# Keys and values of a non-local attention layer: splitting 192 channels as 128 and 64 instead of 96 and 96

## The chip, the core and the metric

The kernel runs on one core of one Trainium2 chip. A core has five engines that run at the same time, each through its own list of instructions: TensorE (PE in the profile, with PEld for the loading of its stationary operand), VectorE (DVE), ScalarE (ACT), GpSimd (POOL) and SyncE (SP), which here issues most of the DMA transfers. The metric is the device time of one execution in microseconds, as a median of several runs.

## The reference

A batch of 4 images with C = 192 channels and 64 x 64 pixels passes through four layers. Layer 0 is an attention block whose queries come from a deformable convolution, with an MLP. Layer 1 is the non-local attention that the change touches. Layer 2 is an attention over overlapping windows with a gated MLP, and layer 3 a depthwise 3 x 3 convolution whose weights depend on the image. Layer 1, with 96 inner channels and N = 4096 pixels:

```python
g_x     = _conv1x1(x, g_w, g_b).reshape(B, O, N)          # O = 96
theta_x = _conv1x1(x, theta_w, theta_b).reshape(B, O, N)
phi_x   = _conv1x1(x, phi_w, phi_b).reshape(B, O, N)
f1 = jnp.einsum('bon,bom->bnm', theta_x, phi_x)
f_div_C = jax.nn.softmax(f1, axis=-1)
y = jnp.einsum('bnm,bom->bon', f_div_C, g_x).reshape(B, O, H, W)
return _conv1x1(y, W_w, W_b) + x
```

So for each image the keys phi (96 x 4096) and the values g (4096 x 96) have to be there in full before the first score can be weighted.

## The kernel before

An image is worked through layer by layer, and the four images follow one another. All data are float32. A matmul on TensorE contracts over partitions: `lhsT` is loaded as the stationary operand and `rhs` is streamed through it. In float32 each matmul appears in the trace as two PE instructions.

**Keys and values.** `keys(b, ph, gx, sb, ps)` makes them for image b. It goes over the 4096 pixels in NCH = 8 chunks of CN = 512. For each chunk one DMA (L865) loads the tile `xk` with the 192 channels as two groups of P = 96 partitions. Two matmuls (L868) contract over 96 + 96 channels and give 96 x 512 of phi in one PSUM bank (`tp`). ScalarE adds the bias and writes it into `ph` (L869). Eight matmuls (L873) give g with pixels on the partitions: four blocks of 128 pixels, each contracted over 96 + 96 channels, side by side in one bank (`g`). VectorE copies them into `gx` (L876). Then the generator yields.

**Who runs beside it.** For images 0 and 3 the chunks follow one another alone, with 4 buffers for `xk`. For images 1 and 2 the driver alternates chunk by chunk with `offsets(b + 1)`, the norm and the offset convolution of the next image's layer 0, with 2 buffers. `offsets` loads its own chunk `xi` (L431), takes mean and variance on TensorE (L360 pm, L339 pv, with ScalarE's squares L367), turns them back into rows (L348 pb), transposes the normed pixels (L462 pt) into a table in DRAM (L466) and writes the normed image (L471). When all eight chunks are done it runs the convolution for the offsets (L482 po, L490 pp) and computes the sampling positions (L494) and indices (L515). After it, `layer1` runs for image b: theta (L912), scores (L920), softmax and weighting (L986). Woven into it is the gather of the next image by indirect DMAs on GpSimd (L572). [...]in images 1 and 2 `offsets` holds 6 and `keys` has 2 (pool `l1kps`).

**The order on each engine.** The program is written as generators in a fixed order, but a list scheduler then orders the instructions of all engines, with tile pools deciding when a buffer is free. DMAs that are given to `in_turn` keep their written order. The weights of layer 1 (`phiT`, `gT`) are loaded by `late()` in `constants()` (L178), one DMA each, on SP's queue.

**Names that come up.** `M`, `Q` = 128, 64; `HN` = 256; `half(q)` = the partitions 64q to 64q + 63; `bass.ts(i, n)` = columns i n to (i + 1) n. fc1 of the MLP (`mlp0`, L803 and L810) contracts over 192 channels as 128 and 64. L693 is a matmul that does no work of the reference: it is issued in idle stretches of TensorE. L1787 and L1793 are layer 3's sums on VectorE and its output stores on SP, which for images 1, 2 and 3 are the last work ahead of `keys`.

Of the kernel before, what the change touches and what calls it, by code (L numbers as in the profile page):

```python
# [10 lines left out]
F32 = mybir.dt.float32  # L11
I32 = mybir.dt.int32
AF = mybir.ActivationFunctionType
ALU = mybir.AluOpType
AX = mybir.AxisListType
PSUM = bass.MemoryType.PSUM
DRAM = bass.MemoryType.DRAM

B, C, H, W = 4, 192, 64, 64
HW = H * W  # L20
P = 96
# [3 lines left out]
M, Q = 128, 64  # L25
NCH = 8
CN = HW // NCH
HN = CN // 2
# [51 lines left out]
def conv_seq_kernel(ctx: ExitStack, tc: tile.TileContext, a, out: bass.AP):  # L80
    nc = tc.nc

    def pool_of(**kw):

        return tc.tile_pool(**({} if kw.get("space") == DRAM else {"reuse_waits": "tile"}), **kw)
# [7 lines left out]
    def const(shape, name):  # L93
        return wpool.tile(shape, F32, tag=name, name=name)
# [8 lines left out]
    V, VW = {}, {}  # L103
    at = 0
# [67 lines left out]
    def in_turn(dma):  # L172

        tc.keep_in_program_order(dma)

    def late(name, src):
        t = const(list(src.shape), name)
        in_turn(nc.sync.dma_start(out=t, in_=src))  # L178
        return t

    def constants():
# [4 lines left out]
        at = 0  # L186
# [2 lines left out]
            at += m * n  # L189

        yield
        thetaT, phiT, gT = (late(n, a[n].rearrange("(k p) n -> p k n", p=P)) for n in ("thetaT", "phiT", "gT"))
        wW = late("wW", a["wW"])

        yield
# [27 lines left out]
        with pool_of(name="wideps", bufs=1, space=PSUM) as pp:  # L223
            n = sum(n for name, n in _V96 if name in _WIDE)
            wide = const([M, 2, n], "wide")
            p = pp.tile([M, 2, n], F32, tag="p", name="p_wide")
            at = 0
            for name, n in _V96:
                if name in _WIDE:
                    cols = slice(at, at + n)  # L230
# [13 lines left out]
        with pool_of(name="foldq", bufs=1, space=PSUM) as pp:  # L244
            p = pp.tile([128, 2, 512], F32, tag="p", name="p_qkv")
            n = 3 * C // 2
# [13 lines left out]
        with pool_of(name="outb", bufs=1, space=PSUM) as pp:  # L260
            p = pp.tile([P, 2], F32, tag="outb", name="pob")
# [6 lines left out]
        bias = const([128, 3, 2, WS * WS], "bias")  # L268
# [3 lines left out]
        with pool_of(name="rpb", bufs=1) as rp:  # L272
            shifted = rp.tile([WS, HEADS, N1 * N1], F32, tag="shifted", name="shifted")
            n = N1 * N1 - WS + 1
            for iy in range(WS):
                in_turn(nc.sync.dma_start(
                    out=shifted[iy : iy + 1, :, 0:n],
                    in_=a["rpb"][:, WS - 1 - iy : WS - 1 - iy + n].unsqueeze(0),
# [22 lines left out]
        for c in range(0, 32, HEADS):  # L301
            n = min(HEADS, 32 - c)
# [14 lines left out]
    with pool_of(name="zero", bufs=1) as zp:  # L317
        zero = zp.tile([128, 4 * C], F32, tag="zero", name="zero")
        nc.gpsimd.memset(zero, 0.0)
        for i in range(2):  # L320
            t = dram.tile([TROWS, 4 * C], F32, tag=f"table{i}", name=f"table{i}")
# [8 lines left out]
    x_flat = [dram.tile([C, HW], F32, tag=f"xd{i}", name=f"xd{i}") for i in range(2)]  # L330
    xn_drams, x_drams = ([t.rearrange("(k p) n -> p k n", p=P) for t in ts] for ts in (xn_flat, x_flat))
# [56 lines left out]
    def links(steps, upto=None):  # L388

        while True:  # L390
            try:
                link = next(steps)
                if upto is not None and link == upto:
                    return None
            except StopIteration as end:
                return end.value
# [462 lines left out]
    def keys(b, ph, gx, sb, ps):  # L859

        nc.gpsimd.memset(gx[:, :, P : P + 1], 1.0)
        for i in range(NCH):
            cols = bass.ts(i, CN)
            x = sb.tile([P, 2, CN], F32, tag="x", name=f"xk_{b}_{i}")
            nc.sync.dma_start(out=x, in_=x_drams[b % 2][:, :, cols])  # L865
            p = ps.tile([128, CN], F32, tag="k", name=f"tp_{b}_{i}")[:P]
            for k in range(2):
                nc.tensor.matmul(p, lhsT=phiT[:, k, :], rhs=x[:, k, :], start=k == 0, stop=k == 1)  # L868
            nc.scalar.activation(ph[:, cols], p, AF.Identity, bias=V["l1_phib"])  # L869
            p = ps.tile([128, CN], F32, tag="k", name=f"g_{b}_{i}")[:, : 4 * P].rearrange("p (j c) -> p j c", j=4)  # L870
            for j in range(4):
                for k in range(2):
                    nc.tensor.matmul(  # L873
                        p[:, j, :], lhsT=x[:, k, bass.ts(j, 128)], rhs=gT[:, k, :], start=k == 0, stop=k == 1
                    )
            nc.vector.tensor_copy(gx[:, bass.ts(i, 4), 0:P], p)  # L876
            yield


# [452 lines left out]
    def of_pair(x, j):  # L1332

        return x[:, bass.ts(j, UN)].rearrange("p (h n) -> p h n", h=2), x[:, 4 * UN + CN * j : 4 * UN + CN * j + CN]

    def half(h):
        return slice(Q * h, Q * h + Q)
# [458 lines left out]
    def rest(b, x, others, oi, sums, m2):  # L1796


        with ExitStack() as s:
            alone = m2 is None  # L1800
            sb = s.enter_context(pool_of(name="norms", bufs=1))
            ps = s.enter_context(pool_of(name="restps", bufs=2, space=PSUM))
            wide = s.enter_context(pool_of(name="restps2", bufs=5, space=PSUM))
            psums = Psums({"n": ps, "v": ps, "h": wide}, {"t": "h"})
            other = iter(())
            if not alone:
                other = mlp0(b + 1, m2, s.enter_context(pool_of(name="l0d", bufs=1)), sb, psums)
            credit = 0.0

            def main():  # L1810
                hn = []

                def ahead():
                    hn.append(links(pair_norm_steps(x, 0, sb, psums, f"l2n2_{b}_0")))

                yield from project(b, x, others, oi.pop(), psums, HFT_PE if alone else (), ahead)
                yield from mlp(b, x, sums, sb, psums, GATE_PE if alone else (), hn)
                yield from layer3(b, x, sums, psums, alone)

            for part in main():  # L1820
                credit += part
                while credit >= 1.0:
                    next(other, None)
                    credit -= 1.0
            for _ in other:
                pass

    def weave(b, at, m2):


        def begin(s):
            parts = gather(b, s, at, m2)
            done = 0

            def go(step):
                nonlocal done
                upto = GATHER_STEPS + 1 if step is None else min(GATHER_STEPS + 1, (GATHER_STEPS + 1) * step // (NQ * NG - 6))
                while done < upto:
                    done += 1
                    next(parts, None)  # L1840

            return go

        return begin
# [13 lines left out]
    with ExitStack() as s:  # L1858
        sb = s.enter_context(pool_of(name="l0first", bufs=1))
        m2 = stats.tile([M, C + 3 * M], F32, tag="m2", name="m2_0")  # L1860
        kept = sb.tile([128, NT, C], F32, tag="kept", name="kept")
        at = links(offsets(0, sb, kept))
# [11 lines left out]
    with ExitStack() as s:  # L1874
        sb, pool = (s.enter_context(pool_of(name=n, bufs=1)) for n in ("norms0", "l0d0"))
        ps = s.enter_context(pool_of(name="l0dps", bufs=2, space=PSUM))
# [3 lines left out]
    for b in range(B):  # L1880
        with ExitStack() as s:
            sb = s.enter_context(pool_of(name="l1x", bufs=1))
            ph = sb.tile([P, HW], F32, name=f"ph_{b}", tag="ph")
            gx = sb.tile([128, HW // 128, P + 1], F32, name=f"gx_{b}", tag="gx")
            beside, m2, at = None, None, at_second
            if b + 1 < B:
                m2 = stats.tile([M, C + 3 * M], F32, tag="m2", name=f"m2_{b + 1}")
            with ExitStack() as s2:
                making = keys(
                    b, ph, gx, s2.enter_context(pool_of(name="l1k", bufs=2 if 0 < b < B - 1 else 4)),  # L1890
                    s2.enter_context(pool_of(name="l1kps", bufs=2, space=PSUM)),
                )
                if 0 < b < B - 1:
                    parts = offsets(b + 1, sb)
                    for _ in range(NCH):
                        next(parts)
                        next(making, None)
                    at = links(parts)
                for _ in making:
                    pass  # L1900
            if b + 1 < B:
                beside = weave(b + 1, at, m2)
            layer1(b, (ph, gx), beside)
        begun.close()
        sums = stats.tile([M, 12], F32, tag="sums", name=f"sums_{b}")
        x = big.tile([M, UNITS * UN + 2 * 2 * 10 * (W + 2)], F32, tag="x", name=f"x_{b}")
        others = x[:, UNITS * UN :].rearrange("p (v k r c) -> p v k r c", v=2, k=2, c=W + 2)

        def load_image():
            for j in range(NCH // 2):  # L1910
                lo, hi = of_pair(x, j)
                for h in range(2):
                    of = x_flat[b % 2][:, bass.ts(2 * j + h, CN)]
                    nc.sync.dma_start(out=lo[:, h], in_=of[0:M])
                    nc.sync.dma_start(out=hi[half(h)], in_=of[M:C])

        oi = big.tile([P, 2, HW], F32, tag="x", name=f"oi_{b}")
        windows(b, oi, load_image)
        held = [oi]
        del oi  # L1920
        rest(b, x, others, held, sums, m2)
        del x, others
# [74 lines left out]
```

## Time and profile before

| | |
|---|---|
| median of 3 runs | 6832.62 us (6821.38 to 6850.82) |
| the profiled execution | 6953.4 us, span 6951.6 us, mean granted TensorE clock 0.938 |
| TensorE busy | 6255.4 us, 90% |
| VectorE, ScalarE, GpSimd busy | 69%, 54%, 30% |
| phi matmuls (L868), 128 instructions | 85.6 us busy |
| g matmuls (L873), 512 instructions | 82.7 us busy |
| `xk` loads (L865) | 32 of 384 KB |
| keys of image 0, alone | 859.9 to 907.7 us |
| keys of image 1 with offsets of image 2 | first phi at 2398.8 us, indices at 2514.4 us |
| keys of image 2 with offsets of image 3 | first phi at 4023.8 us, indices at 4134.2 us |
| keys of image 3, alone | 5640.2 to 5692.1 us |

All but the first row come from one profiled execution, which was 1.8% longer than the median. A share of the span is an average over very different stages; what matters for this change are the four stages in the last rows. A row such as `L868 PE MATMUL tp<-xk,phiT 96*96 96x512` names the line, the engine, the tiles written and read, the rows and columns of the stationary operand and the shape of the result. After it come the count, the busy time in us, the mean of one in ns, and how long the engine was idle just before these instructions and what ended that wait. Matmuls are pipelined, so a mean of 795 ns doesn't say that one can start only every 795 ns: the distance of their starts says that.

### The profile page before, as it was taken

Reading aid. Unit: us, or ns where it says so; the run is one execution under the profiler, and the core shown is the slowest. Engines: PE = TensorE matmul, PEld = TensorE weight load, DVE = VectorE, ACT = ScalarE, POOL = GpSimd, SP = SyncE. Lnnn points to the kernel's source line nnn. Section 1 sums busy time; section 2 is a strip of 40 time slices with the busy share of each in tenths; the row PEclk is TensorE's granted clock in tenths of the full one; section 3 lists DMA queues with packets and bytes.
Section 4 is the critical chain, followed back from the end, with each engine's and each line's share of the span. In section 5 each row is a group of like instructions: output and inputs, shape, how many; then the busy total and the mean of one; then the engine's idle time right before and its main releaser. Section 6 shows DMA issues by size and latency. Waiting matters only on the chain.

```text
span 6951.6 us, 115213 instructions
## 1 busy us (share of the span) xinstructions
PE 6255.4 (90%) x45188; PEld 4235.5 (61%) x45188; DVE 4817.8 (69%) x7087; ACT 3725.4 (54%) x6214; POOL 2061.6 (30%) x2273
## 2 busy tenths in 40 slices
PE   7677999999988899999988899999998889999876
PEld 4445578886643468886654458887554457766432
DVE  3664279985577769985586849996576757765656
ACT  3664368874544358874544348885544325545331
POOL 2654057752200047761200017772210000012100
PEclk8888989999999999999989999999998979999988
DMA  7795257751010277762010067673110010010000
GB/s 229 257 317 180 70 161 225 226 180 36 21 28 13 62 237 227 220 214 57 11 42 12 21 216 217 220 222 102 32 29 22 14 52 10 14 36 12 7 3 20
DMA packets 362109, 743.45 MB, mean 107 GB/s; under 512 B 52647, under 2 KB 245335, under 8 KB 360798
## 3 DMA queue, kind: packets, MB, share of 16 engines
q0 software_dynamic: 95616, 469.38, 21.1%
q1 hardware_dynamic: 265950, 266.70, 12.9%
q8 instruction: 356, 5.83, 0.4%
q14 instruction: 187, 1.53, 0.1%
HBM read 628.06 MB, written 106.21 MB: 106 GB/s over the span
## 4 chain that ended last, share of the span: by engine, by line
PE 65%; DVE 17%; ACT 7%; issue 4%; DMA 4%; SPq 1%; another core or an unknown queue 1%; POOL 1%; DVEq 0%; ACTq 0%; POOLq 0%
PE s L920 11%; PE y L986 11%; PE h L590 7%; PE v L1151 2%; DVE ha L1328 2%; PE qk L1076 2%; PE h L1528 2%; DMA ring<-table,idx 2%; PE qk L1077 2%; DVE ga L1328 2%; PE po L482 2%; PE t L1159 1%; PE h L803 1%; DVE gate L1328 1%; PE zm L1539 1%
## 5 line engine op out<-in xcount | busy, mean ns | idle before, releaser
L572 POOL DMA_INDIRECT ring<-table,idx x1188 | 1657.7, 1395 | 1103.3 <-DVE row L579 273.2
L920 PE MATMUL s<-ths,ph 96*128 96x256 f32 x4096 | 981.6, 385 | 14.2 <-ACT ths L914 7.4
L920 PEld LDWEIGHTS s<-ths,ph 96*128 96x128 f32 x4096 | 782.8, 193 | 154.8 <-ACT ths L914 19.0
L578 ACT ACTIVATE row<-ring,pos 128x384 f32<-128x384 f32 x1188 | 697.7, 609 | 213.5 <-DVE xo L583 132.4
L579 DVE SCALAR_TENSOR_TENSOR row<-ring,fr,row 128x384 f32<-128x384 f32 x1188 | 696.9, 611 | 84.1 <-ACT row L578 56.8
L986 PE MATMUL y<-sc,gx 128*97 128x256 f32 x3008 | 720.1, 379 | 0.0
L582 ACT ACTIVATE xo<-row,pos 128x192 f32<-128x192 f32 x1188 | 504.6, 448 | 151.3 <-remote 73.1
L986 PEld LDWEIGHTS y<-sc,gx 128*97 128x97 f32 x3008 | 489.0, 164 | 125.7 <-issue 2.3
L583 DVE SCALAR_TENSOR_TENSOR xo<-row,fr,xo 128x192 f32<-128x192 f32 x1188 | 464.4, 411 | 106.9 <-ACT xo L582 59.6
L590 PE MATMUL h<-ti,xo 128*128 128x192 f32 x2376 | 460.3, 329 | 5.6 <-DVE xo L583 5.6
L922 ACT COPY sc<-s 128x1024 f32<-128x1024 f32 x376 | 377.3, 1003 | 164.1 <-PE s L920 155.1
L983 DVE TENSOR_TENSOR sc<-sc,mbs 128x1024 f32<-128x1024 f32 x376 | 446.7, 1216 | 20.9 <-ACT mbs L946 13.7
L927 DVE TENSOR_TENSOR top<-top,sc 128x1024 f32<-128x1024 f32 x282 | 344.5, 1222 | 149.5 <-ACT sc L922 133.9
L590 PEld LDWEIGHTS h<-ti,xo 128*128 128x128 f32 x2376 | 404.4, 191 | 40.4 <-DVE xo L583 11.7
L984 ACT ACTIVATE sc<-sc 128x1024 f32<-128x1024 f32 x376 | 392.5, 1053 | 39.2 <-DVE sc L983 36.6
L1135 DVE TENSOR_REDUCE es<-ex 128x6 f32<-128x384 f32 x264 | 133.3, 546 | 358.8 <-ACT ex L1131 358.8
L590 PE MATMUL h<-kept,xo 128*128 128x192 f32 x990 | 261.9, 402 | 121.4 <-DVE xo L583 61.7
L1569 POOL COPY gate<-gate 128x192 f32<-128x192 f32 x12 | 4.2, 351 | 1115.2 <-ACT gate L1562 1115.2
L590 PEld LDWEIGHTS h<-kept,xo 128*128 128x128 f32 x990 | 191.2, 226 | 203.6 <-DVE xo L583 92.9
L1328 DVE SCALAR_TENSOR_TENSOR ga<-gate,v,ga 128x1024 f32<-128x1024 f32 x234 | 299.7, 1281 | 7.2
L986 PE MATMUL y<-se,gx 128*97 128x256 f32 x1088 | 260.4, 379 | 0.5 <-ACT yn L992 0.5
L1533 ACT ACTIVATE z<-h,bias_fc1T 128x512 f32<-128x512 f32 x192 | 118.0, 687 | 230.2 <-PE h L1530 229.9
(390 smaller groups left out, 11548.6 us busy)
## 6 DMA issues: line engine op xcount, KB each, us to landing
ti<-table SPq DMA_DIRECT2D x396, 96.0 KB
table<-tt SPq DMA_DIRECT2D x24, 1056.0 KB
ring<-table,idx POOLq DMA_INDIRECT x1188
xnd<-xn SPq DMA_DIRECT2D x4, 3270.0 KB
table<-kept SPq DMA_DIRECT2D x12, 1056.0 KB
table<-tt SPq DMA_DIRECT2D x44, 288.0 KB
xi<-in_x_dram SPq DMA_DIRECT2D x32, 384.0 KB
xk<-xd SPq DMA_DIRECT2D x32, 384.0 KB
```

Of the source, the lines that this page charges most:

```text
L572: nc.gpsimd.indirect_dma_start(out=gt.rearrange("p r q c -> p (r q c)"), out_offset=None, in_=table[:, :], in_offset=bass.IndirectOffsetOn ...
L578: nc.scalar.activation(row, gt[:, :, 0, :], AF.Copy, scale=pos[:, t, 9 + tap : 10 + tap])
L579: nc.vector.scalar_tensor_tensor(row, gt[:, :, 1, :], fr[:, t, 9 + tap : 10 + tap], row, ALU.mult, ALU.add)
L582: nc.scalar.activation(xo[:, j, :], row[:, 0, :], AF.Copy, scale=pos[:, t, tap : tap + 1])
L583: nc.vector.scalar_tensor_tensor(xo[:, j, :], row[:, 1, :], fr[:, t, tap : tap + 1], xo[:, j, :], ALU.mult, ALU.add)
L590: nc.tensor.matmul(acc[m // 2][:, bass.ts(m % 2, C)], lhsT=xo.rearrange("p j c -> p (j c)")[:, bass.ts(m, 128)], rhs=tt, start=t == 0 and ...
L920: nc.tensor.matmul(p[:, t, :], lhsT=ph[:, bass.ts(G * g + t, 128)], rhs=ths[i], start=True, stop=True)
L922: nc.scalar.copy(to, p)
L983: nc.vector.tensor_tensor(ex, ex, mbs[i].unsqueeze(1).to_broadcast([128, G, QN]), ALU.add)
L984: nc.scalar.activation(ex, ex, AF.Exp)
L986: nc.tensor.matmul(py, lhsT=gx[:, G * g + t, :], rhs=ex[:, t, :], start=g == 0 and t == 0, stop=g == NG - 1 and t == G - 1,)
L1328: nc.vector.scalar_tensor_tensor(acc[:, b], src(tap, b), w[:, tap : tap + 1], acc[:, b], ALU.mult, ALU.add)
```

## The change

The 192 channels are split as 128 and 64 instead of 96 and 96. Channels 0 to 127 of a chunk lie on all 128 partitions, 512 columns wide. Channels 128 to 191 of the chunk's first 256 pixels lie on partitions 0 to 63, those of its second 256 pixels on partitions 64 to 127, in 256 further columns. The weights are laid out in the same way, with the last 64 rows once on each half. So a chunk takes three loads instead of one, and the two weights take three each.

Phi becomes four matmuls of 256 columns: 128 channels for each half of the pixels, into two PSUM banks, and then 64 channels for each, on different halves of the partitions. g takes eight matmuls as before, for two blocks j: 128 channels for both halves, then 64 channels for both. Each result is in two banks, and so there are two evictions of half the size on ScalarE and two copies on VectorE. `l1kps` has 4 buffers for images 0 and 3, and 2, as before, for images 1 and 2.

```diff
@@ constants()
-        thetaT, phiT, gT = (late(n, a[n].rearrange("(k p) n -> p k n", p=P)) for n in ("thetaT", "phiT", "gT"))
+        thetaT = late("thetaT", a["thetaT"].rearrange("(k p) n -> p k n", p=P))
+        phiT, gT = const([M, 2, P], "phiT"), const([M, 2, P], "gT")
+        for t, n in ((phiT, "phiT"), (gT, "gT")):
+            in_turn(nc.sync.dma_start(out=t[:, 0, :], in_=a[n][0:M]))
+            for q in range(2):
+                in_turn(nc.sync.dma_start(out=t[half(q), 1, :], in_=a[n][M:C]))
@@ keys()
+        image = x_flat[b % 2]
         for i in range(NCH):
-            cols = bass.ts(i, CN)
-            x = sb.tile([P, 2, CN], F32, tag="x", name=f"xk_{b}_{i}")
-            nc.sync.dma_start(out=x, in_=x_drams[b % 2][:, :, cols])
-            p = ps.tile([128, CN], F32, tag="k", name=f"tp_{b}_{i}")[:P]
-            for k in range(2):
-                nc.tensor.matmul(p, lhsT=phiT[:, k, :], rhs=x[:, k, :], start=k == 0, stop=k == 1)
-            nc.scalar.activation(ph[:, cols], p, AF.Identity, bias=V["l1_phib"])
-            p = ps.tile([128, CN], F32, tag="k", name=f"g_{b}_{i}")[:, : 4 * P].rearrange("p (j c) -> p j c", j=4)
-            for j in range(4):
-                for k in range(2):
+            x = sb.tile([M, 3 * HN], F32, tag="x", name=f"xk_{b}_{i}")
+            nc.sync.dma_start(out=x[:, 0:CN], in_=image[0:M, bass.ts(i, CN)])
+            for q in range(2):
+                nc.sync.dma_start(out=x[half(q), CN:], in_=image[M:C, bass.ts(2 * i + q, HN)])
+            banks = [ps.tile([128, CN], F32, tag="k", name=f"tp_{b}_{i}_{q}")[:P, 0:HN] for q in range(2)]
+            for q, p in enumerate(banks):
+                nc.tensor.matmul(p, lhsT=phiT[:, 0, :], rhs=x[:, bass.ts(q, HN)], start=True, stop=False)
+            for q, p in enumerate(banks):
+                nc.tensor.matmul(p, lhsT=phiT[half(q), 1, :], rhs=x[half(q), CN:], start=False, stop=True)
+            for q, p in enumerate(banks):
+                nc.scalar.activation(ph[:, bass.ts(2 * i + q, HN)], p, AF.Identity, bias=V["l1_phib"])
+            banks = [
+                ps.tile([128, CN], F32, tag="k", name=f"g_{b}_{i}_{q}")[:, 0 : 2 * P].rearrange("p (j c) -> p j c", j=2)
+                for q in range(2)
+            ]
+            for j in range(2):
+                for q, p in enumerate(banks):
+                    at = HN * q + 128 * j
+                    nc.tensor.matmul(p[:, j, :], lhsT=x[:, at : at + 128], rhs=gT[:, 0, :], start=True, stop=False)
+                for q, p in enumerate(banks):
+                    at = CN + 128 * j
                     nc.tensor.matmul(
-                        p[:, j, :], lhsT=x[:, k, bass.ts(j, 128)], rhs=gT[:, k, :], start=k == 0, stop=k == 1
+                        p[:, j, :], lhsT=x[half(q), at : at + 128], rhs=gT[half(q), 1, :], start=False, stop=True
                     )
-            nc.vector.tensor_copy(gx[:, bass.ts(i, 4), 0:P], p)
+            for q, p in enumerate(banks):
+                nc.vector.tensor_copy(gx[:, bass.ts(2 * i + q, 2), 0:P], p)
             yield
@@ the driver
-                    s2.enter_context(pool_of(name="l1kps", bufs=2, space=PSUM)),
+                    s2.enter_context(pool_of(name="l1kps", bufs=2 if 0 < b < B - 1 else 4, space=PSUM)),
```

## Prediction

> **What bounds the kernel now.** I read the page's busy times first, to see which engine is short:
>
> ```profile
> span 6951.6 us, 115213 instructions
> PE 6255.4 (90%) x45188; PEld 4235.5 (61%) x45188; DVE 4817.8 (69%) x7087; ACT 3725.4 (54%) x6214; POOL 2061.6 (30%) x2273
> ```
>
> TensorE (PE) is 90% busy. That is an average, so next come the groups of the two lines that change, with shapes kept apart, and of the gated MLP's fc1 (L803, L810), which already works as the change would: 128 channels, then 64 on each half of the partitions.
>
> ```profile
> L868 PE MATMUL tp<-xk,phiT 96*96 96x512 f32 x128 | 85.6, 795 | 6.7 <-DMA xk<-xd 5.6 <-ACT ph L869 0.9
> L873 PE MATMUL g<-gT,xk 96*128 96x96 f32 x512 | 82.7, 328 | 0.0
> L869 ACT ACTIVATE ph<-tp,v 96x512 f32<-96x512 f32 x32 | 21.9, 683 | 159.6 <-PE tp L868 137.5 <-issue 17.1 <-PE g L873 5.0
> L803 PE MATMUL h<-d_l0m,fc 128*128 128x256 f32 x768 | 206.9, 413 | 16.7 <-DVE d_l0m L749 14.5 <-ACT z L1533 2.2
> L810 PE MATMUL h<-d_l0m,fc 64*128 64x256 f32 x768 | 113.3, 408 | 0.0
> ```
>
> The changed lines hold 85.6 + 82.7 = 168.3 us of PE: 2.4% of the span, so no outcome is large. ACT's eviction waits 137.5 us for PE and PE 0.9 us for ACT: PE sets the pace. The chain of waits says whether these stages are on the path, and what a chunk takes. First it passes L803/L810 ahead of image 0's keys, then two chunks, then (after "...") two later half-chunks:
>
> ```profile
> 840.16 1.92 PE h L803 x8
> 842.08 1.06 PE h L810 x8
> ...
> 860.08 1.72 PE tp L868 x4
> 861.80 1.76 PE g L873 x16
> ...
> 878.88 3.36 PE g L873 x16
> 882.24 3.41 PE tp L868 x4
> ```
>
> A chunk is 1.72 + 1.76 = 3.48 us early and 3.36 + 3.41 = 6.77 us later: same instructions, double time. The windows show why (the columns are sum, then PE, PEld, DVE, ACT, POOL busy, granted clock, DMA share, GB/s); image 0, image 3, image 1, image 2:
>
> ```profile
> 868.00:905.00 37.00, 36.74 (x104) 23.61 (x105) 3.35 (x6) 3.62 (x6) 0.94 (x1) 0.50 0.30 89
> 5650.00:5680.00 30.00, 30.00 (x90) 20.16 (x90) 2.79 (x5) 2.73 (x4) 0.00 (x0) 0.50 0.17 46
> 2412.00:2449.00 37.00, 36.50 (x249) 23.69 (x248) 17.74 (x24) 17.13 (x24) 0.00 (x0) 1.00 0.34 97
> 4022.00:4069.00 47.00, 45.15 (x284) 28.38 (x283) 18.90 (x25) 18.66 (x27) 0.00 (x0) 1.00 0.44 127
> ```
>
> PE is full in all four. Images 0 and 3 (keys alone, 859.9 to 907.7 and 5640.2 to 5692.1) run at clock 0.50; images 1 and 2, where chunks alternate with the offsets of the next image, run at 1.00. In images 1 and 2 the stage ends when PE has done the offset convolution, then L494, then the indices L515 (2514.4 and 4134.2), which release the first gather (2515.7 and 4135.6). So every PE microsecond in any of the four stages moves the end.
>
> [...]
>
> ```profile
> 5616.66 1.99 PE L803 MATMUL h<-d_l0m,fc 128*128 128x256 f32 x8
> 5618.59 1.13 PE L810 MATMUL h<-d_l0m,fc 64*128 64x256 f32 x8
> 5619.65 0.70 PE L803 MATMUL h<-d_l0m,fc 128*128 128x256 f32 x2
> ```
>
> Listed singly, the L810 instructions start in pairs 6 ns apart. So a pair takes one slot of 1.72/8 = 0.215 us (256 columns; 512 took 1.72/4). Eight slots and four slots would be 1.72 and 0.86 us, but the starts lie 1.93 and 1.06 us apart: **each switch between 128 and 64 rows costs 0.20 us**. [...] PE is full for 37 us at 0.50. [...]
>
> **The change part by part.** Per matmul PE runs two instructions (x16 for 8 matmuls of g).
>
> Removed: half of the streaming of 64 rows. In slots, phi was 4 x 0.43 = 1.72 us and becomes 4 + 2 slots of 0.215 = 1.29; g was 16 x 0.11 = 1.76 and becomes 12 x 0.1115 = 1.34. A chunk would be 2.63 instead of 3.48 us, 25% less.
>
> Added: switches. In the written order phi has 2, and g has 4. Phi's cost 0.20. For g the last-to-first gap in the trace between the shapes puts one near 0.16. Sum 0.40 + 0.64 = 1.04, so a chunk is 3.67: **0.19 us longer, not shorter**, at full clock. At half clock the same gaps around L803/L810 are 0.30 per phi switch, and I take 0.24 for g's: (6 x 0.427 + 0.60) + (12 x 0.213 + 0.96) = 6.68 against 6.77, no change within 0.2.
>
> Images 0 and 3 had 3 chunks at full clock and 13 at half: +0.6 and -1.2. Four PSUM buffers instead of two remove the one wait for the eviction (0.7 us at 867.5). Image 3: its xk_3_0 now needs two more loads, which SP issues behind the output stores L1793, as it did only xk_3_1 before; that second load reached PE at 5645.7 with 1.52 us of PE idle. Now PE waits in chunk 0 instead, so +2 (0 to +4). Together 0.6 - 1.2 - 0.7 + 2 = +1.
>
> Images 1 and 2: the compiled order splits the pairs. A chunk is tp 128 twice; the offsets' pv; tp 64 twice; then g 128, 64, 128 for one half and again for the other, then 64, 64 together, with the offsets' pb, pm, pt and po between. Switches rise from 44 to 110 a stage (the offsets have their own). Cost: 66 x 0.20 = 13.2. Saved: per chunk 0.43 on phi, and on g 16 - 14 slots of 0.11 (one of its two pairs of matmuls stays together) = 0.22; 8 x 0.65 = 5.2. Net **+8.0 an image**. These two keep two PSUM buffers for twice as many tiles, so g's first half waits for phi's eviction (0.47 us for 96x256 at L914), partly filled by the offsets: 0.2 to 0.5 a chunk, +3. As in image 3, the two 64-row loads of the first chunk come behind two L1793 stores on SP: +2. Sum +13 an image (6 to 20), **+26 for both**. DVE's and ACT's two half-size evictions are hidden behind PE (ACT 17.1 of 37 us busy); unhidden, the second would be 0.47 us a chunk, which the next rival prices.
>
> Loads: 96 issues instead of 32 on SP, plus 6 for 2 of the weights. Shares of DMA of 0.17 to 0.44 in the four windows leave room except at a stage's first chunk, counted above. The knock-on in the first 640 us, where the weights are loaded during the gather of image 0: -3 to +3, taken as 0. Order moves by the scheduler elsewhere on SP (L471 now ahead of a table write L466): 0 +-2.
>
> Clock: [...] A lift saves 6.77 - 3.67 = 3.1 us for each chunk left, 0 to 20 an image. I take -4 an image[...]: -8.
>
> Total: 1 + 26 - 8 = **+19 us**. The profiled execution is 6953.4 (span 6951.6), 1.8% above the median 6832.62; the sum is made on its rows and added to the median, as neither clock nor PE fill of these stages suggests that they differ between executions: 6852.
>
> **Rivals.**
> (A) *The clock lifts early in images 0 and 3*: 6 chunks x 3.1 x 2 = -37, with +27 elsewhere: about -10, 6823. [...] Against: PE full at 0.50 for 37 us[...].
> (B) *The two PSUM buffers become the bound of images 1 and 2*, the slower side: four tiles pass through two banks per chunk, so phi's eviction (0.47) and then g's copy stand between PE's steps, with ACT also queued behind the offsets' squares (L367). At 1.0 us for each of 16 chunks +16, with another 0.7 for ACT's queue +11, on +16 of switches and +4 of loads; A's clock absent: +40 to +50, 6877. It decides once a chunk loses over 0.9 us beyond its switches. For: PE waits already 0.9 us for ph with two tiles a chunk. Against: offsets' matmuls stand between in the compiled order.
> (C) *The switches cost nothing here* (smaller weights, other order): -0.65 for each of 16 chunks in images 1 and 2, -0.85 for 3 at full clock and -1.65 for 13 at half = -34; if those 13 run at full clock too, 6.77 - 2.63 each, -67. About -48: 6785. For: the diff's arithmetic. Against: 0.20 us at each switch of L803/L810.
> (D) *Images 1 and 2 do not do what the change says*, since the order splits the pairs: already in the forecast.
>
> **How the numbers follow.** Main case 0.52, own range +5 to +36 (6838 to 6869); A 0.15; B 0.25; C 0.08. A measurement here tells about 0.5%, 34 us, from no change. Low end 6800 takes in A and part of C; high 6893 takes in B with its upper bound. Faster by over 0.5%: C and a tail of A with cheap middle images, 0.10. Slower by over 0.5%: B and the top of the main case, 0.32. The rest 0.58.
>
> **What would show it.** Right: L803-like gaps of 0.2 us at each change of rows in keys; first phi to L515 of images 1 and 2 rises from 115.6 and 110.4 us (2398.8 to 2514.4, 4023.8 to 4134.2) by about 13; images 0 and 3 stay near 48 and 52 us. A shows as clock 1.00 in 868 to 905; B as idle of PE ahead of g released by ACT ph; C as a chunk of 2.6 us. A stage of images 1 and 2 that does not lengthen, or a shift of over 10 us outside the four stages, would prove me wrong.

## The result and the profile after

| | before | after |
|---|---|---|
| median of 20 runs each | 6828.84 us (6803.38 to 6863.79) | 6862.93 us (6841.1 to 6875.7) |
| ratio | | 1.0053, 95% interval 1.0039 to 1.0066 |
| the profiled execution's span, clock | 6951.6 us, 0.938 | 6873.9 us, 0.944 |

The change costs 34 us (27 to 45). The two profiled executions say the opposite, 78 us less: the one of before was far longer than its timed runs. So the profiles are compared stage by stage, and more profiles of each form of `keys` are needed (below).

First the groups of the page's kind, shapes apart, of the kernel after. L876 and L878 are phi with 128 and with 64 rows, L888 and L891 the same for g, L880 is phi's eviction:

```profile
L888 PE MATMUL g<-gT,xk 128*128 128x96 f32 x256 | 51.4, 305 | 3.8 <-ACT ph L880 3.8
L891 PE MATMUL g<-gT,xk 64*128 64x96 f32 x256 | 40.0, 320 | 0.0
L876 PE MATMUL tp<-xk,phiT 128*96 128x256 f32 x128 | 39.1, 426 | 1.6 <-DVE gx L895 0.9 <-DMA xk<-xd 0.7
L880 ACT ACTIVATE ph<-tp,v 96x256 f32<-96x256 f32 x64 | 27.2, 466 | 131.7 <-PE tp L878 131.6
L878 PE MATMUL tp<-xk,phiT 64*96 64x256 f32 x128 | 25.6, 431 | 3.9 <-DMA xk<-xd 3.9
```

The four PE groups add to 156.1 us busy where it was 168.3. That is no gain yet: part of the fall is clock, and the time that passes at a switch of rows shows in no group. It has to be read from the starts. One chunk of image 0 in the timeline after, and the first line of the next:

```profile
841.10 1.10 PE L876 MATMUL tp<-xk,phiT 128*96 128x256 f32 x4
842.14 0.68 PE L878 MATMUL tp<-xk,phiT 64*96 64x256 f32 x4
842.74 0.69 PE L888 MATMUL g<-gT,xk 128*128 128x96 f32 x4
843.36 0.47 PE L891 MATMUL g<-gT,xk 64*128 64x96 f32 x4
843.75 0.69 PE L888 MATMUL g<-gT,xk 128*128 128x96 f32 x4
844.37 0.47 PE L891 MATMUL g<-gT,xk 64*128 64x96 f32 x4
844.76 1.10 PE L876 MATMUL tp<-xk,phiT 128*96 128x256 f32 x4
```

A chunk is 844.76 - 841.10 = **3.66 us**; the prediction had 3.67, and before it was 3.48 at full clock. Listed singly, the L878 instructions start in pairs 7 ns apart. So the pairs do run side by side, and the switches eat more than that saves.

The windows after, image 0, image 3, image 1, image 2 (columns as before):

```profile
819.00:849.00 30.00, 30.00 (x197) 20.14 (x196) 4.82 (x16) 6.66 (x16) 7.17 (x8) 1.00 0.66 228
5590.00:5622.00 32.00, 30.93 (x199) 21.09 (x197) 4.97 (x16) 6.73 (x16) 0.00 (x0) 1.00 0.40 119
...
2335.00:2375.00 40.00, 36.66 (x209) 21.89 (x210) 11.56 (x18) 14.23 (x28) 0.00 (x0) 0.91 0.39 110
3956.00:3996.00 40.00, 37.41 (x149) 20.88 (x149) 7.84 (x13) 9.83 (x18) 0.00 (x0) 0.66 0.30 87
```

Images 0 and 3, which were at clock 0.50, are at 1.00 and take 29.2 and 30.4 us instead of 47.6 and 51.5. Images 1 and 2 are worse: first phi to the end of the indices takes 125.4 and 134.6 us instead of 116.1 and 110.9, and in image 2 the first 40 us have a clock of 0.66. The four stages of these two profiles together are 6.5 us shorter after, while the medians are 34 us apart. What belongs to the change and what to one execution is what the experiments had to separate.

### The profile page after: what moved, and what is told of

Read it like the earlier page. It is cut to its first block, busy times and chain, and to the rows that moved or that the text cites. A ratio compares the mean times of both kernels' runs of the same rounds, so it can differ in the third digit from the quotient of the medians.

```text
span 6873.9 us, 115637 instructions
## 1 busy us (share of the span) xinstructions
PE 6218.3 (90%) x45316; PEld 4208.6 (61%) x45316; DVE 4822.6 (70%) x7119; ACT 3736.6 (54%) x6246; POOL 2084.7 (30%) x2273
## 4 chain that ended last, share of the span: by engine, by line
PE 65%; DVE 19%; ACT 7%; DMA 5%; issue 4%; POOL 0%; SPq 0%; DVEq 0%; ACTq 0%; POOLq 0%
PE s L939 12%; PE y L1005 10%; PE h L595 6%; DMA ring<-table,idx 3%; PE v L1170 2%; PE po L487 2%; DVE ha L1347 2%; PE qk L1095 2%; PE h L1547 2%; PE qk L1096 2%; DVE ga L1347 2%; PE t L1178 1%; DVE gate L1347 1%; PE zm L1558 1%; PE rb L1244 1%
## 5 line engine op out<-in xcount | busy, mean ns | idle before, releaser
L577 POOL DMA_INDIRECT ring<-table,idx x1188 | 1683.1, 1417 | 1028.3 <-ACT sc L941 307.8
L1218 POOL TENSOR_TENSOR ot<-ot,ot 102x128 f32<-102x128 f32 x80 | 55.8, 711 | 626.1 <-ACT ot L1212 610.4
```

Of the source, the lines that this page charges most:

```text
L577: nc.gpsimd.indirect_dma_start(out=gt.rearrange("p r q c -> p (r q c)"), out_offset=None, in_=table[:, :], in_offset=bass.IndirectOffsetOn ...
```

## The experiments

My theory was the forecast's: switches of rows cost what the halved streaming saves, and more in images 1 and 2. Against it: the two PSUM banks (rival 2 in the texts below, B in the prediction), the three loads (rival 3), and the clock. All stages in one table, in us: images 0 and 3 from first phi to first theta, images 1 and 2 from first phi to the end of L515's indices. Each stage comes from one profiled execution; where there is no ratio, the kernel ran only once. An asterisk marks at least 35 us of the stage at half clock.

| kernel | image 0 | image 1 | image 2 | image 3 | ratio to before (95%) |
|---|---|---|---|---|---|
| before | 47.6* | 116.1 | 110.9 | 51.5* | |
| after | 29.2 | 125.4 | 134.6 | 30.4 | 1.0053 (1.0039 to 1.0066) |
| ends only | 29.2 | 111.4 | 113.7 | 30.3 | 0.9990 (0.9972 to 1.0008) |
| middle only | 28.1 | 130.0 | 131.9 | 51.4* | 1.0076 (1.0050 to 1.0103) |
| 96 + 96, two banks | 28.0 | 114.0 | 116.6 | 29.3 | 1.0016 (0.9998 to 1.0033) |
| three loads | 27.9 | 111.6 | 111.1 | 29.4 | 0.9962 (0.9945 to 0.9978) |
| grouped | 26.5 | 111.2 | 110.9 | 28.0 | 0.9991 (0.9975 to 1.0006) |
| other queue | 29.2 | 123.4 | 121.6 | 29.2 | 1.0037 (1.0022 to 1.0053) |
| stall, old then new | 29.0 | 114.0 | 110.9 | 33.1 | |
| stall, new then old | 30.3 | 111.2 | 114.2 | 52.2* | |
| longer stall | 42.4 | 125.4 | 131.4 | 46.5 | |
| three loads, two queues | 27.8 | 110.3 | 110.7 | 27.8 | 0.9973 (0.9959 to 0.9988) |
| three loads again | 27.9 | 111.7 | 111.0 | 29.5 | 0.9969 (0.9955 to 0.9984) |

**The change for images 0 and 3 alone.**

```diff
-                making = keys(
+                making = (keys if b in (0, B - 1) else keys96)(
```

`keys96` is the old function; it takes its first 96 rows of weights from the new tile.

> The change for images 0 and 3 alone; images 1 and 2 keep 96 and 96 channels. Theory 1 (switches between 128 and 64 rows cost what the halved streaming saves, and more where the offsets split the pairs): the keys of images 0 and 3 take 29 to 31 us at full clock, as in the profile after. If the kernel before usually runs these two stages at half clock, as in its one profile (48 and 52 us), the time falls by 35 to 40 us. If it usually runs them at full clock (8 x 3.48 = 28 us), the time changes by 0 to +5. Rival 2 (two PSUM banks in images 1 and 2 are the cost) says the same of this kernel; rival 3 (three loads for each chunk instead of one are the cost) expects about half of the loss, +15.

Measured: 6829.66 us, ratio 0.9990, so -19 to +5 us. The stages are 29.2 and 30.3 us at full clock, as expected. A fall of 35 to 40 us is excluded: the half clock of both stages, as in the one profile of before, isn't what its timed runs usually have. Rival 3's +15 is excluded as well.

**The change for images 1 and 2 alone.**

```diff
-                making = keys(
+                making = (keys if 0 < b < B - 1 else keys96)(
```

> The change for images 1 and 2 alone; images 0 and 3 keep 96 and 96 channels and two PSUM buffers. Theory 1: first phi to indices takes about 125 us in both images where clocks are equal (before: 116 and 111), up to 135 where the half clock at the start lasts; the time rises by 20 to 35 us. If the gain at images 0 and 3 in the profile after was real for usual executions, it must be 60 or more, since the whole change measured +34. The profile also shows a second time which clock images 0 and 3 get in their old form: 48 and 52 us again (the clock belongs to the form), or near 28 (it was chance).

Measured: 6895.57 us, ratio 1.0076, +34 to +70 us. **The whole loss is made here.** Both images take 130 and 131.9 us. The old form got full clock in image 0 and half clock in image 3 (the windows of the two):

```profile
818.00:846.00 28.00, 27.95 (x161) 19.58 (x160) 3.90 (x7) 5.47 (x8) 6.97 (x8) 1.00 0.73 232
5583.00:5634.00 51.00, 49.80 (x159) 33.66 (x158) 3.90 (x7) 5.46 (x8) 0.00 (x0) 0.56 0.25 65
```

So one form can have either clock. The measured +52 is above the 20 to 35 us expected and below the 60 that a usual gain in images 0 and 3 would have asked for; with six runs the interval holds values of both. It also exceeds what the two stages have over the old form's usual 112.8 (+36); the interval reaches down to it.

**96 and 96 channels in the frame of the change.**

```diff
+            banks = [ps.tile(...)[:P, 0:HN] for q in range(2)]
             for k in range(2):
-                nc.tensor.matmul(p, lhsT=phiT[:, k, :], rhs=x[:, k, :], start=k == 0, stop=k == 1)
+                for q, p in enumerate(banks):
+                    nc.tensor.matmul(p, lhsT=phiT[:, k, :], rhs=x[:, k, bass.ts(q, HN)], start=k == 0, stop=k == 1)
...
```

g, evictions, copies and `l1kps` follow the change in the same way, where the dots stand.

> Split 96 and 96 as before, with one load a chunk, but in the frame of the change: phi in four matmuls of 256 columns, two tiles of phi and two of g a chunk, two evictions and two copies of half the size, the same PSUM buffers. No switch of rows and no pairs. Theory 1: nothing is lost but the waits of g for phi's eviction, 2 us an image in the profile after: +0 to +6 us in all, images 1 and 2 at 111 to 119 us. Rival 2 (two banks for four tiles): most of the loss is here, +20 to +35 us, with idle of TensorE ended by ScalarE's ph.

Measured: 1.0016, -1 to +23 us, images 1 and 2 at 114.0 and 116.6: 1 and 4 us over 112.8, the mean of the eight stages of the old form with one load (before, ends only, the two stalls). The waits of TensorE in image 2:

```profile
PE pp L490 <- ACT ot L487: 1.4, 2, 0.7
PE tp L869 <- DMA xk<-xd: 1.2, 1, 1.2
PE tp L869 <- DVE gx L883: 0.2, 1, 0.2
PE pb_l L348 <- DVE r_l L374: 0.2, 1, 0.2
```

No wait for `ph` is among them. By these stages and waits, twice as many tiles in two banks are not the main cost, and rival 2 falls as the main cause. The ratio alone, which reaches to +23 us, wouldn't exclude its +20 to +35.

**Three loads in the old form.**

```diff
-            nc.sync.dma_start(out=x, in_=x_drams[b % 2][:, :, cols])
+            nc.sync.dma_start(out=x[:, 0, :], in_=x_flat[b % 2][0:P, cols])
+            for q in range(2):
+                nc.sync.dma_start(out=x[:, 1, bass.ts(q, HN)], in_=x_flat[b % 2][P:C, bass.ts(2 * i + q, HN)])
```

> The kernel before with three loads a chunk instead of one (96 x 512, then twice 96 x 256). Theory 1: +0 to +5 us, from the first chunk of images 1, 2 and 3, whose last loads stand behind the output stores. Rival 3 (loads): +20 to +35. A third look at the clock of images 0 and 3 in the old form: 48 and 52 us if it belongs to the form, near 28 if it was chance.

Both theories missed the sign: 6815.32 us, ratio 0.9962, **15 to 38 us faster** than before. The start of image 1 shows one place. The timeline of before:

```profile
2398.76 1.96 PE L868 MATMUL tp<-xk,phiT 96*96 96x512 f32 x4
2400.56 1.92 PE L873 MATMUL g<-gT,xk 96*128 96x96 f32 x16
2404.79 3.70 PE L868 MATMUL tp<-xk,phiT 96*96 96x512 f32 x4 [2.31 <-DMA xk<-xd]
```

and with three loads:

```profile
2336.97 0.36 PE L875 MATMUL g<-gT,xk 96*128 96x96 f32 x2
2338.66 0.91 PE L875 MATMUL g<-gT,xk 96*128 96x96 f32 x6 [1.33 <-DMA xk<-xd]
```

One late load of 2.31 us, after which phi takes 3.70 us (half clock), has become one of 1.33 us without it. In image 3 all three profiles of the old form with one load are at half clock (51.5, 51.4, 52.2 us), all three with three loads at full clock (29.4, 29.5, 27.8). The length of the wait doesn't decide it: in image 3 the old form with one load waited for 1.2 to 1.5 us, three loads on one queue for 1.3, and 96 and 96 in two banks, with one load, for 1.15 us and kept full clock as well. What in the three loads keeps the clock is open.

**Fewer switches.**

```diff
             for j in range(2):
-                for q, p in enumerate(banks):   # 128 rows
-                for q, p in enumerate(banks):   # 64 rows
+                for i, q in both:               # 128 rows, both j
+            for j in range(2):
+                for i, q in both:               # then 64 rows, both j
```

The loops over g are shown in short, against those of the change. `both` holds one chunk in image 0 and two in image 3, where phi's matmuls are gathered over both chunks too.

> Images 1 and 2 keep 96 and 96 channels (with three loads a chunk); images 0 and 3 have 128 and 64 with fewer switches. Image 0: all 128-row matmuls of g in a chunk, then all 64-row ones, so 4 switches a chunk instead of 6. Image 3: two chunks together (eight PSUM buffers), so 2 switches a chunk. Theory 1 (0.20 us a switch at phi, 0.16 at g): image 0 from 29.2 to 8 x (3.67 - 0.32) = 26.8 us, image 3 from 30.3 to about 8 x 2.99 + 1 = 25 us. If a switch costs nothing here and something else ate the saving, both stay within 0.5 us of 29.2 and 30.3. The whole time, against the kernel before: -20 to -40, of which most is the half clock of the two stages avoided.

Image 0 took 26.5 us (26.8 expected), with 3.32 us from chunk to chunk. In image 3 two chunks have a period of 5552.02 - 5546.06 = 5.96 us in its timeline, 2.98 a chunk (2.99 expected):

```profile
5546.06 1.11 PE L882 MATMUL tp<-xk,phiT 64*96 64x256 f32 x8
5547.10 2.02 PE L891 MATMUL g<-gT,xk 128*128 128x96 f32 x16
5549.06 1.14 PE L898 MATMUL g<-gT,xk 64*128 64x96 f32 x16
5550.12 1.97 PE L880 MATMUL tp<-xk,phiT 128*96 128x256 f32 x8
5552.02 1.11 PE L882 MATMUL tp<-xk,phiT 64*96 64x256 f32 x8
```

With the same matmuls as in the change and 2 switches instead of 6, a chunk is 0.68 us shorter and beats the old 3.48. **Where the chunks have TensorE to themselves, the switches are the cost, shown:** 3.66, 3.32 and 2.98 us with 6, 4 and 2 of them, 0.17 us each. The stage took 28.0, not 25: two chunks' loads have to be there before the first step, and theta waits for its load at the end. The time, 0.9991, isn't told from before; the expected -20 to -40 was too much. The four stages add to 276.6 us, less than the 280.0 of three loads in the old form, which was faster than before. The stages don't explain that; it stays open.

**The late loads on another queue.**

```diff
-                nc.sync.dma_start(out=x[half(q), CN:], ...)
+                (nc.gpsimd if b and i == 0 else nc.sync).dma_start(out=x[half(q), CN:], ...)
```

> The whole change, but the two 64-row loads of the first chunk of images 1, 2 and 3 go through GpSimd's queue, so that they don't stand behind the output stores L1793 on SP. Theory: in images 1 and 2 the idle of TensorE at the first chunk (1.3 to 1.5 us) drops the clock to half for 7 to 30 us, and that is what makes 125 to 135 us out of about 122. Without it: 120 to 125 us in both images, no half clock in the first 40 us, image 3 at 29.3 us, and the whole time 10 to 20 us under that of the change (+15 to +25 against before). Rival: the idle comes at another chunk (waits for phi's eviction) and the half clock stays, 125 to 135 us.

Measured: 123.4 and 121.6 us as expected; 1.0037, which is +15 to +36 us against before. The first 40 us of images 1 and 2:

```profile
2342.00:2382.00 40.00, 36.58 (x221) 21.61 (x219) 12.90 (x21) 15.65 (x31) 0.00 (x0) 0.96 0.37 107
3963.00:4003.00 40.00, 36.29 (x234) 22.03 (x235) 14.55 (x23) 16.25 (x33) 0.00 (x0) 1.00 0.39 106
```

Clocks of 0.96 and 1.00 stand where the change has 0.91 and 0.66; the 0.96 is one stretch of 3.4 us at half clock, which was not expected. The lost clock accounts for the stages: 0.05 of 40 us is 2.0 us in image 1, 0.34 of 40 us is 13.6 in image 2, and the stages are 2.0 and 13.0 us shorter than with the change. So a load that is 1.3 to 1.5 us late costs little by itself; the half clock that follows costs 2 to 13 us an image. The wait alone doesn't bring it: with three loads in the old form TensorE waits 1.2 to 1.5 us at the same place of images 1 and 2, and the clock fell in the first 40 us of none of six stages (three loads twice, grouped); with the change and its loads on SP (after, middle only, longer stall) it fell in six of six. At full clock the change still costs 10 us an image. Where they go is shown by the waits of TensorE in image 2, here:

```profile
PE g L888 <- ACT ph L880: 3.0, 8, 0.7
PE pp L495 <- ACT ot L492: 2.1, 3, 0.7
PE tp L876 <- DVE gx L895: 1.4, 2, 1.0
PE pb_l L353 <- DVE r_l L379: 0.2, 1, 0.2
```

and with 96 + 96 and three loads:

```profile
PE pp L490 <- ACT ot L487: 1.4, 2, 0.7
PE g L875 <- DMA xk<-xd: 1.3, 1, 1.3
PE po L482 <- ACT ot L487: 0.4, 1, 0.4
PE pm_l L360 <- DMA xi<-in_x_dram: 0.2, 1, 0.2
```

The stages are 121.6 and 111.1 us, 10.5 apart; the waits add to 6.7 and 3.3, so 3.4 of it is waiting (phi's eviction, in each of the 8 chunks, has 3.0), and the remaining 7.1 is put down to matmuls and switches.

**A forced wait, both ways round.** Images 1 and 2 are in the old form.

```diff
-            nc.scalar.activation(ph[:, cols], p, AF.Identity, bias=V["l1_phib"])
+            for _ in range(6 if i == 2 and b in (0, B - 1) else 1):
+                nc.scalar.activation(ph[:, cols], p, AF.Identity, bias=V["l1_phib"])
```

> A wait of about 4 us of TensorE is forced after chunk 2 in images 0 and 3 (the eviction of phi's chunk 2 is repeated six times, same data): image 0 in the old form, image 3 in the new one; images 1 and 2 in the old form. It shows how each form gets on once the clock has fallen to 0.50. Theory [...]: the old form stays at 0.50 to the end of its keys, about 44 us; the new form comes back to 1.00 within two or three chunks, about 38 us. Rival (the form doesn't matter): both stay at 0.50, or both come back.

> The same forced wait with the forms exchanged: image 0 in the new form, image 3 in the old one. Theory: image 0 comes back to clock 1.00 within two or three chunks, image 3 stays at 0.50 to the end. Rival: what happens goes by the image and not by the form.

Inconclusive as designed: the repeated evictions overlapped with g, TensorE waited 0.4 to 0.65 us and not 4, and no clock fell from that. But the late loads of image 3 made one try in each. The new form (33.1 us) was at half clock for one stretch of 3.4 us and came back; the old form (52.2 us) fell after 6.3 us and stayed to the end.

**A longer wait in the change.** The same with twelve evictions, in the whole change.

> The whole change, with phi's eviction of chunk 2 repeated twelve times in images 0 and 3, so that TensorE stands still for 4 to 6 us ahead of chunk 3 there. In seven profiles the old form, alone on TensorE, fell to clock 0.50 four times and never came back before its end; the new form fell once, for one window of 3.4 us. Theory (form decides): in both images the clock falls to 0.50 after the wait and is at 1.00 again within 10 us, the stages take 36 to 42 us. Rival (it was chance, a longer wait holds the new form down as well): 0.50 to the end of the keys, 50 us or more.

The wait was 4.33 us, and both clocks fell. In the timeline of image 0, phi of chunks 4, 5 and 6:

```profile
830.58 1.17 PE L889 MATMUL g<-gT,xk 128*128 128x96 f32 x4 [4.33 <-ACT ph L881]
...
834.13 2.02 PE L876 MATMUL tp<-xk,phiT 128*96 128x256 f32 x4
...
840.73 2.02 PE L876 MATMUL tp<-xk,phiT 128*96 128x256 f32 x4
...
847.33 1.98 PE L876 MATMUL tp<-xk,phiT 128*96 128x256 f32 x4
849.25 0.68 PE L878 MATMUL tp<-xk,phiT 64*96 64x256 f32 x4
```

A chunk at half clock is 840.73 - 834.13 = 6.60 us (6.68 in the prediction, 6.77 in the old form). The clock came back at about 849 us, after 20.5 us, and in image 3 after 27 us. The old form, alone on TensorE, fell four times. Three falls, all in image 3, lasted to the end of the keys, 54.6 us in the kernel before. The fourth, in image 0 of the kernel before, lasted 37.5 us and ended with the last chunk:

```profile
902.35 3.57 PE L868 MATMUL tp<-xk,phiT 96*96 96x512 f32 x4
905.75 1.92 PE L873 MATMUL g<-gT,xk 96*128 96x96 f32 x16
907.51 1.03 PE L912 MATMUL th<-xc,thetaT 96*96 96x256 f32 x4
```

From start to start this phi takes 3.40 us and this g 1.76, half clock and then full. So the old form did come back once, against what the expectation says. The new form came back in all three of its falls alone on TensorE, but only by the third to fourth chunk after the long wait and not within 10 us, and the stages (42.4 and 46.5) are longer than expected. That the form decides fits; with so few falls, after waits of different lengths, it isn't shown.

**The old form with three loads, and the first chunk's on two queues.** The two edits above together, on the old form; and three loads alone once more.

> The kernel before with three loads a chunk, and for the first chunk of images 1, 2 and 3 the last two of them on GpSimd's queue. Theory (what is to be had here is to keep TensorE from standing still at the first chunks, so that the clock isn't lost): image 1 and 2 at 109 to 111 us, image 3 at 28 us, no half clock in the first 40 us of any of the four stages; the time 20 to 35 us below the kernel before. Rival: without the wait the old form still loses its clock in image 3 in about half of the executions, and the time is 5 to 15 below.

> The kernel before with three loads a chunk, all on SP, once more: it measured 0.9962 of before (0.9945 to 0.9978). Theory: 10 to 30 us below before again, stages of 28, 111, 111 and 29 us without half clock. If the first time was chance: within 5 us of before, image 3 at 50 us.

Two queues: 0.9973 (8 to 28 us faster), stages at 27.8, 110.3, 110.7 and 27.8, no half clock in their first 40 us. The 18 us lie between the theory's 20 to 35 and the rival's 5 to 15 and decide for neither. Three loads again: 0.9969 (11 to 31 faster), as expected. **Both beat the kernel before**, and so the change, and can't be told from each other.

## Why the prediction was right, and where its steps were off

The median lies 11 us above the forecast, within the range; of the cost itself the forecast had 19 of 34 us. Whether the change costs more than 0.5%, which the prediction gave 0.32, the interval of 0.39% to 0.66% leaves open.

**The switch.** Right in kind, and in size as a sum. A chunk at full clock 3.66 against 3.67, at half clock 6.60 against 6.68, and "fewer switches" hit 26.8 and 2.99 with 26.5 and 2.98. The single prices were a little off and cancel: with 2.63 us of streaming, 1.03 us are left for six switches, 0.17 each in phi as in g, where the prediction had 0.20 and 0.16. That g's matmuls of 128 rows and pairs of 64 take the slot of those of 96 was an estimate of mine; in image 3 of "fewer switches" 16 and 8 slots of g, each with a switch, take 1.96 and 1.06 us from start to start, so 0.11 a slot and 0.16 a switch. At half clock it is (6.60 - 5.12) / 6 = 0.25, for 0.30 and 0.24. Rival C is excluded.

**Images 1 and 2 at full clock.** Switches and split pairs +8.0, waits for phi's eviction +3: the runs show 7.1 and 3.4, the first of them as a remainder. A control agrees with it. With half of the time at half clock taken off, as an estimate, all eight stages with the change take 121 to 122 us; 96 and 96 with the same tiles, banks and evictions, but no change of rows, takes 114.0 and 114.9, so 7 are left for what the rows do. The first chunks split even phi, as the timeline after shows (image 1):

```profile
2352.47 0.67 PE L876 MATMUL tp<-xk,phiT 128*96 128x256 f32 x2
2353.07 0.67 PE L878 MATMUL tp<-xk,phiT 64*96 64x256 f32 x2
2353.67 0.67 PE L876 MATMUL tp<-xk,phiT 128*96 128x256 f32 x2
2354.27 0.67 PE L878 MATMUL tp<-xk,phiT 64*96 64x256 f32 x2
```

Each step of 0.60 us is two slots of 0.215 and a switch of 0.17.

**The late first load: the term that was mis-sized.** I put it at +2 an image, its waiting time. The wait itself is no longer than what the old form had at its second chunk. The trace of before held a warning: its wait of 2.31 us in image 1 is followed by half clock from 2404.2 to 2411.0 us, and the prediction's window, from 2412 on, left that out. What the late load costs is the clock: the six stages with the change and its loads on SP (after, middle only, longer stall) average 129.8 us, the two with the other queue 122.5. So it is about +7, and an image loses about 17 against the old form with one load (112.8), not 13.

**The clock in images 0 and 3.** I took one profile for the usual state, saw no sign that these stages differ between executions, and put 13 chunks at half clock and a cautious -8 for a lift, an estimate: no trace of before showed what lifts the clock. The sign that these stages stay near 48 and 52 us failed, and the half clock in image 0, which I read over 37 us and took to last, ended at 905.7. The change does keep full clock, in seven of its eight stages without the longer wait; the eighth lost 3.4 us. But the old form with one load has it in image 0 in two of three profiles too; in image 3 it lost it in three of three. By stages, ends only should thus give -20 or more; it measured -7, at most -19. That 1 - 8 = -7 was also the forecast for these two images is luck: its clock term was made for stages that usually start at half clock.

Timed runs show their mean clock. As an estimate, 1 less this clock, times the run's time, is the time lost to the clock. Against the runs of before beside it, ends only loses 17 us less, middle only 34 us more, the other queue 6 us more, and three loads lose 16 and 20 us less (all give or take 10, middle only 17). So the gain of three loads, 26 and 21 us, is mostly clock. Ends only does gain clock and pays about 10 us elsewhere. Of the 52 us of middle only about 18 are not clock, and of the 25 with the other queue about 19, which is the 10 us an image found above. Which stage of a timed run loses the clock isn't seen.

**The sum.** 2 x 17 = +34 for images 1 and 2, about -7 for 0 and 3 as measured, gives +27, at the lower end of 27 to 45. What remains could lie in the first 810 us, where the weights take more loads: the first phi starts at 811 to 819 us in the eight profiles that load the new layout, and at 802 to 812 in the four others beside before. These overlap, and it is left open. A shift of over 10 us outside the four stages was named as a sign of being wrong. Between the two profiles it is 71 us, but it is the one of before that stands apart: 6625 us outside the stages, where the twelve others have 6522 to 6557. A shift of 10 us can't be told in that.

**Rivals.** A's mechanism, full clock in images 0 and 3, happened in the profile, but didn't bring its time, since the old form is often there as well. B's waits exist, but PE waits 3.8 us for phi's eviction in the whole kernel after (L888 in the first list), 2.4 and 3.0 us in images 1 and 2 with the other queue, and not 16.

## What to carry to other kernels

Two matmuls of 64 rows side by side save half of their streaming (here a pair starts 7 ns apart and takes one slot), but each change between 128 and 64 rows costs 0.17 us, most of a slot of 256 columns (0.215); count the switches in the order that is really issued, and gather all of one kind before the other kind starts. Where another stage was woven in, with two PSUM banks, the pairs were split and the switches rose from 44 to 110, so such a change belongs, if anywhere, where TensorE works alone and banks are free. Even there it made no kernel here faster than before (0.9990 and 0.9991). A load that is late by a microsecond or two at the start of a matmul stage should be weighed by the clock that it may cost (2 to 13 us an image here, after waits of 1.3 to 1.5 us), and cutting it in parts so that the first matmuls can start is worth trying by itself.

## What the runs showed of the hardware

- Float32 matmuls of 64 rows on the two halves of the partitions started 7 ns apart in pairs (L878 of the kernel after). A change between 128 and 64 rows cost 0.17 us at full clock (a chunk of 3.66 us in the kernel after) and 0.25 us at half clock (6.60 us with the longer stall), with 256 columns streamed as with 96.
- The granted clock fell to 0.50 within 5 us of waits of TensorE of 0.93, 2.31 and 1.52 us (before: images 0, 1 and 3), of 1.50 and 1.35 us (after: images 1 and 2) and of 4.33 us (longer stall, image 0). It didn't after 0.93 us in image 2 of before, 1.07 us in image 3 of after and 1.33 us in image 1 with three loads.
- Alone on TensorE, 96 rows stayed at 0.50 once for 37.5 us, and then came back (before, image 0), and for 54.6 us in image 3 of before; two more stretches, in image 3 of middle only and of "stall, new then old", lasted to the end of the keys. Alternating 128 rows with pairs of 64 came back after 3.4 us ("stall, old then new", image 3), and after 20.5 and 27 us (longer stall, images 0 and 3). What decides is open.
- A busy TensorE alone didn't bring the clock back within these stretches: it was busy for 18.42 of 19 us at 0.50 with the longer stall (830 to 849 us), and for 53.44 of 54 us at 0.50 in image 3 of before (5647 to 5701 us).
- A single load of 384 KB cut into three was faster for the kernel by 11 to 38 us in two comparisons (0.9962 and 0.9969), by an estimate from the runs' mean clock mostly because less clock was lost. Why the clock holds is not shown.
